# One-hots of edge places moved from the even to the odd half steps of a graph layer on one Trainium2 core

## The chip, the core and the metric

The kernel runs on one core of a Trainium2 chip. The core has five engines that run side by side: TensorE (PE in the profile, with PEld for its weight loads), VectorE (DVE), ScalarE (ACT), GpSimd (POOL) and SyncE (SP). The metric is the device time of one execution in microseconds (us). Lower is better.

## The reference

One layer of a graph network over 12,500 nodes with 128 features and 400,000 edges, which are sorted by their destination. Cut to what matters:

```python
h = relu(layernorm(x))                                  # 12500 x 128
m = relu(concat(h[src], h[dst], edge_attr) @ w1 + b1) @ w2 + b2
agg = segment_sum(m, dst, 12500)
gi, gh = agg @ w_ih + b_ih, h @ w_hh + b_hh             # a GRU cell per node
r = sigmoid(gi_r + gh_r); z = sigmoid(gi_z + gh_z); n = tanh(gi_n + r * gh_n)
out = x + (1 - z) * n + z * h
```

## The kernel before

**Tables.** A first part makes h transposed for all nodes (`hT_all`, kept in SBUF) and a table A = h @ w1[0:128] in HBM, so that the source's share of an edge's product is a row of A.

**Pairs and halves.** The 3,125 tiles of 128 edges are taken in 391 pairs `k` of up to eight tiles (two groups of four: the "double group"). Each pair is worked off in two half steps: `u = 2k` (even) and `u = 2k + 1` (odd), with four tiles each. The main loop runs over `u`, and each engine executes its instructions in the order in which this loop writes them; no scheduler moves them.

**What one pair needs.**

- Eight gathers on GpSimd (`gather`, L144), each an indirect DMA of 128 rows of A by the numbers in `src_i` into the pair's tile G. Twelve such tiles are to be had at the start and eight later; 18 of the 391 pairs are not gathered but fetched column by column out of `hT_all` by ScalarE (L775) and VectorE (L777). That makes 2,981 gathers.
- The transposed one-hot of the destination nodes (`onehot_T`, L493): VectorE compares the destination numbers of 512 edges, which a DMA has spread over 64 partitions, with each partition's node number, and writes 64x512 floats into L.
- The product of this one-hot and of the edge attributes with RW (`pre`, L590), on TensorE. RW holds the destination's share, made from a window of `hT_all` by `window` (L512, L515) and `window_rows` (L524).
- The one-hot of the edges' places in the window (`onehot`, L542): VectorE compares `dloc` (16 bits, one place per edge) with `iota` (16 bits, 0 to 31), both in SBUF, and writes 128x256 floats into one of six OH tiles.
- `add` (L615): G += product, on VectorE, once a half's four gathers have landed. `relu` (L621) on ScalarE writes RB.
- `seg` (L634) on TensorE sums RB by OH into PSUM, and `take` (L642, L643) copies the sums out.
- Every fourteen pairs, a block of 512 nodes goes through the GRU cell (`node`, L650 to L723), spread over later halves.

**The order on VectorE.** In an even half: some of the L777 copies, the copy L642 of the pair before, the compares L493 and L542 for the pair three ahead, the add L615 of the half two ahead; then L512, more L777 and the two L524. In an odd half: L777, the add L615, L777. The one-hot of places for pair k + 3, made in half 2k, is first read by `seg` in half 2k + 6.

**The order on GpSimd.** In the main part it issues gathers alone. `gathers` asks for them as far ahead as the G tiles allow.

Of the kernel before, what the change touches and what calls it, by code (L numbers as in the profile page):

```python
# [54 lines left out]
def tile_gnn(ctx: ExitStack, tc: tile.TileContext, x, src, srcT, dstT, dstP, eaT, eaP, w1, b1, w2T, b2,  # L55
# [15 lines left out]
    def tiles(k):  # L71
        return (0 if k == 0 else SUP0 + (k - 1) * PAIR, SUP0 + k * PAIR)
# [416 lines left out]
    def onehot_T(k):  # L489
        if k >= NP:  # L490
            return
        c = slice((k % QP) * 512, (k % QP + 1) * 512)
        nc.vector.tensor_scalar(Ls[k // QP][:2 * V, c], Ds[k // QP][:, c], node_of[:, k:k + 1],  # L493
                                None, op0=ALU.is_equal)
# [31 lines left out]
    def onehot(k):  # L526
        if k >= NP:
            return
        t0, t1 = tiles(k)
        OH[k] = OHB[k % len(OHB)]  # L530
        for a in range(2) if k == 0 else (None,):
            if a is None:
                o, s = OH[k].rearrange("p j a v -> p a j v"), slice(t0, t1)
                d = dloc[:, s].rearrange("p (a j) -> p a j", a=2)[:, :, :, None]
                shape = [128, 2, GRP, V]
                i = iota[:, None, None, :]
            else:
                e = min(t1, (a + 1) * GRP)
                o, d = OH[k][:, :e - a * GRP, a, :], dloc[:, a * GRP:e, None]
                shape = [128, e - a * GRP, V]  # L540
                i = iota[:, None, :]
            nc.vector.tensor_tensor(o, d.to_broadcast(shape), i.to_broadcast(shape),  # L542
                                    op=ALU.is_equal)
# [9 lines left out]
    def raw_h(u):  # L553
        if u < 2 * RAW:
            for i, s in enumerate(slots(u)):
                relu_norm(unit(u)[:, s, :], unit(u)[:, s, :], HE[u][:, i, :])

    def raw_stats(u):
        if u < 2 * RAW:
            l = slots(u)  # L560
            HE[u] = bn_sqrt(p2, bn(p2, lambda j: unit(u)[:, l[j], :], 128, len(l)), 128, len(l))

    def raw_fin(u):
        if u < 2 * RAW:
            n = len(slots(u))
            st = p2.tile([128, GRP, 2], F32, name="st_raw", bufs=4)
            bn_fin(p2, st[:, :n, :], HE[u], 128, n)
            HE[u] = st

    def raw_turn(u):  # L570
        if u < 2 * RAW:
            l = slots(u)
            pt = ps1.tile([128, 512], F32, name="misc")
            for i, s in enumerate(l):
                nc.tensor.transpose(pt[:, i * 128:(i + 1) * 128], unit(u)[:, s, :], ident)
            hT = p3.tile([128, 512], F32, name="hTe", bufs=2)
            nc.vector.tensor_copy(hT[:, :len(l) * 128], pt[:, :len(l) * 128])
            HE[u] = hT
# [3 lines left out]
    def pre(u):  # L582
        if u >= NU:
            return
        k, h = divmod(u, 2)
        PP[u] = ps2.tile([128, GRP, D], F32, name="pre")
        for i in range(2):
            c0 = (k % QP) * 512 + (2 * h + i) * 128
            raw = u in HE or k in hand
            nc.tensor.matmul(PP[u][:, 2 * i:2 * i + 2, :], Ls[k // QP][:, c0:c0 + 128], RW[k % 4],  # L590
                             start=True, stop=not raw)
            if raw:
                l = unit_tiles(u)
                for n, (t, j, a) in enumerate(l):
                    if j % 2 == i:
                        if k in hand:
                            c = (a * GRP + j) * 128
                            cols = hand[k][:, c:c + 128]
                        else:
                            cols = HE[u][:, n * 128:(n + 1) * 128]  # L600
                        nc.tensor.matmul(PP[u][:, 2 * i + a, :], cols, w1a, start=False,
                                         stop=n + 1 == len(l) or l[n + 1][1] != j)


    def add(u):
        if u >= NU:
            return
        if u in HE or u // 2 in hand:
            RT[u] = PP.pop(u)
            HE.pop(u, None)  # L610
            if u % 2:
                hand.pop(u // 2, None)
        else:
            RT[u] = unit(u)
            nc.vector.tensor_tensor(RT[u], PP.pop(u), RT[u], op=ALU.add)  # L615

    def relu(u):
        if u >= NU:
            return
        o = RB[u % 3]  # L620
        nc.scalar.activation(o[:, :, :D], RT.pop(u), AF.Relu)  # L621
        if u % 2:
            G.pop(u // 2, None)
# [207 lines left out]
    def stages(u):  # L831
        if u + 7 >= 0:
            raw_stats(u + 7)
        if u + 6 >= 0:
            raw_fin(u + 6)
            raw_h(u + 6)
        if u % 2 == 0:
            onehot_T(u // 2 + 3)
            onehot(u // 2 + 3)
        if u + 4 >= 0:  # L840
            raw_turn(u + 4)
        if u + 3 >= 0:
            pre(u + 3)
        if u + 2 >= 0:
            add(u + 2)
            relu(u + 2)

    for u in range(-7, 0):
        stages(u)
# [12 lines left out]
    for u in range(NU):  # L862
# [29 lines left out]
        if h == 0:  # L892
            take(k - 1)
        stages(u)
        other(1)
        other(2)
# [177 lines left out]
```

## Time and profile before

| | us |
|---|---|
| median of 3 runs | 3845.28 (3842.6 to 3846.54) |
| the profiled execution's own time | 3851.33 |
| its span, first to last instruction | 3849.6 |

| engine | busy us | share of the span | instructions |
|---|---|---|---|
| POOL | 2895.7 | 75% | 2989 |
| PE | 2660.6 | 69% | 13274 |
| DVE | 2007.8 | 52% | 12309 |
| ACT | 1650.1 | 43% | 11720 |

The profile shows one execution, instruction by instruction, with start and duration. "Busy" counts the instruction's own duration; what an engine spends between instructions, waiting or issuing, is listed as idle time before the next one, with what ended it. The word "issue" stands there for time in which the engine waited for nothing that the profile shows. L144 is line 144 of the kernel.

### The profile page before, as it was taken

The page shows a single profiled execution, that of the slowest core. Times are in us where ns is not written, and L with a number is a line of the kernel's source. Part 1 is how long each engine was busy: PE and PEld are TensorE (multiplying, and loading weights), DVE is VectorE, ACT ScalarE, POOL GpSimd, SP SyncE. Part 2 cuts the span into 40 slices and gives each one's busy share as a digit, 9 for nine tenths or more (in the row PEclk, how much of TensorE's full clock was granted, in tenths as well). Part 3 has the DMA queues.
Part 4 walks back from the last instruction along what each step waited for, and adds up shares of the span by engine and source line. Part 5 has one row for each costly group of instructions (what it writes and reads, how often), then busy time and mean ns, then how long its engine had stood idle before and what let it go on. Part 6 is the DMA issues. An engine that isn't in the chain of part 4 may idle for free. (4 is left out here: it accounts for less than half of the span.)

```text
span 3849.6 us, 62154 instructions
## 1 busy us (share of the span) xinstructions
PE 2660.6 (69%) x13274; PEld 1624.1 (42%) x13274; DVE 2007.8 (52%) x12309; ACT 1650.1 (43%) x11720; POOL 2895.7 (75%) x2989
## 2 busy tenths in 40 slices
PE   6688766766775675776777577666667766775776
PEld 6554443443443443443444344433434443443443
DVE  7766655544545444554555455455545545544432
ACT  5446544444444444443544444444444444444311
POOL 7777777777777777777777777777777777777774
PEclk9888777777777777776777787687867777777776
DMA  6343333333333333333333333333333333333331
GB/s 202 87 99 93 85 91 84 77 87 82 88 82 87 82 84 85 84 86 79 90 84 83 81 88 87 77 92 78 89 80 89 77 87 82 89 80 85 88 81 38
DMA packets 151695, 333.68 MB, mean 87 GB/s; under 512 B 62088, under 2 KB 68019, under 8 KB 151317
## 3 DMA queue, kind: packets, MB, share of 16 engines
q0 software_dynamic: 95392, 195.55, 20.1%
q1 hardware_dynamic: 55781, 134.06, 13.5%
q8 instruction: 110, 1.80, 0.2%
q14 instruction: 268, 2.20, 0.2%
q10 hardware_dynamic: 144, 0.07, 0.0%
HBM read 315.60 MB, written 13.84 MB: 86 GB/s over the span
## 5 line engine op out<-in xcount | busy, mean ns | idle before, releaser
L144 POOL DMA_INDIRECT G<-A,src_i x2904 | 2821.9, 972 | 886.8 <-issue 837.3
L590 PE MATMUL pre<-RW,L 128*128 128x256 f32 x3128 | 1164.7, 505 | 120.4 <-DVE G L615 107.5
L775 ACT COPY HE_act<-hT_all 128x4 uint8 x10240 | 1055.5, 188 | 380.8 <-issue 378.9
L621 ACT ACTIVATE RB<-G 128x512 f32<-128x512 f32 x726 | 456.9, 629 | 1409.2 <-DVE G L615 1099.0
L615 DVE TENSOR_TENSOR G<-pre,G 128x512 f32<-128x512 f32 x726 | 499.8, 688 | 890.4 <-DMA G<-A,src_i 876.2
L515 PE MATMUL oh<-w1b,hw 128*64 128x128 f32 x782 | 217.1, 370 | 1019.8 <-DVE hw L512 1014.0
L590 PEld LDWEIGHTS pre<-RW,L 128*128 128x128 f32 x3128 | 696.7, 246 | 435.2 <-issue 311.3
L777 DVE TENSOR_REDUCE HE_dve<-hT_all 128x4 uint8 x8192 | 641.3, 148 | 359.8 <-issue 354.2
L634 PE MATMUL seg<-RB,OH 128*32 128x129 f32 x6250 | 657.4, 346 | 6.0 <-ACT dcol L643 4.4
L515 PEld LDWEIGHTS oh<-w1b,hw 128*64 128x64 f32 x782 | 92.6, 168 | 1184.2 <-DVE hw L512 1154.0
L634 PEld LDWEIGHTS seg<-RB,OH 128*32 128x32 f32 x6250 | 356.3, 133 | 256.6 <-issue 139.9
L524 DVE TENSOR_TENSOR RW<-oh,b1b 32x128 f32<-32x128 f32 x782 | 218.9, 280 | 171.8 <-PE oh L515 164.8
L642 DVE COPY sums<-seg 64x128 f32<-64x128 f32 x391 | 108.5, 278 | 211.0 <-PE seg L634 207.1
L493 DVE TENSOR_SCALAR L<-Ld,node_of 64x512 f32<-64x512 int32 x391 | 193.9, 496 | 0.1
L643 ACT CAST dcol<-seg 64x1 f16<-64x1 f32 x391 | 59.6, 152 | 261.2 <-DVE sums L642 259.0
L665 PEld LDWEIGHTS nd<-spot,sums 64*128 64x128 f32 x782 | 164.4, 321 | 13.8 <-issue 13.8
L665 PE MATMUL nd<-spot,sums 64*128 64x40 f32 x782 | 168.5, 404 | 0.0
L542 DVE TENSOR_TENSOR OH<-dloc,iota 128x256 f32<-128x256 f16 (+1 forms) x392 | 160.0, 408 | 0.0
L629 PE MATMUL seg<-zrow 1*64 1x129 bf16 x391 | 107.1, 274 | 0.0
L512 DVE COPY hw<-hT_all 128x64 f32 x391 | 85.3, 218 | 18.2 <-issue 7.0
L144 POOL DMA_INDIRECT G<-in_x,src_i x77 | 72.8, 946 | 24.9 <-issue 22.8
L629 PEld LDWEIGHTS <-zrow 1*64 1x64 bf16 x391 | 43.6, 111 | 97.4 <-issue 97.4
(147 smaller groups left out, 1366.4 us busy)
## 6 DMA issues: line engine op xcount, KB each, us to landing
L<-in_eaP SPq DMA_DIRECT2D x195, 256.0 KB
Ld<-in_dstP SPq DMA_DIRECT2D x390, 128.0 KB
G<-A,src_i POOLq DMA_INDIRECT x2904
xb<-in_x SPq DMA_DIRECT2D x28, 256.0 KB
out<-xb SPq DMA_DIRECT2D x28, 256.0 KB
xs<-in_x SPq DMA_DIRECT2D x11, 512.0 KB
A<-asb SPq DMA_DIRECT2D x11, 512.0 KB
src_i<-in_srcT SPq DMA_DIRECT2D x19, 80.0 KB
```

What stands on the lines that cost most here:

```text
L144: nc.gpsimd.indirect_dma_start(out=G[k][:, j, a, :], out_offset=None, in_=table, in_offset=bass.IndirectOffsetOnAxis(ap=src_i[c][:, i:i + ...
L493: nc.vector.tensor_scalar(Ls[k // QP][:2 * V, c], Ds[k // QP][:, c], node_of[:, k:k + 1], None, op0=ALU.is_equal)
L515: nc.tensor.matmul(PB_[k][:2 * V, :D], hw.rearrange("p a v -> p (a v)"), w1b, start=True, stop=True)
L524: nc.vector.tensor_tensor(RW[k % 4][s, a, :], pm[s, :D], b1b[s, :], op=ALU.add)
L542: nc.vector.tensor_tensor(o, d.to_broadcast(shape), i.to_broadcast(shape), op=ALU.is_equal)
L590: nc.tensor.matmul(PP[u][:, 2 * i:2 * i + 2, :], Ls[k // QP][:, c0:c0 + 128], RW[k % 4], start=True, stop=not raw)
L615: nc.vector.tensor_tensor(RT[u], PP.pop(u), RT[u], op=ALU.add)
L621: nc.scalar.activation(o[:, :, :D], RT.pop(u), AF.Relu)
L634: nc.tensor.matmul(SEG[k][V * a:V * (a + 1), :D + 1], OH[k][:, j, a, :], RB[u % 3][:, (j % 2) * 2 + a, :D + 1], start=False, stop=all(b != ...
L665: nc.tensor.matmul(pt[:, bass.ds(offs[i], V + SHIFT)], sums[:, i, :], spot, start=False, stop=i == n - 1)
L775: nc.scalar.copy(he[:, e * 4:e * 4 + 4], h_bytes[:, bass.ds(v - H_AT, 4)])
L777: nc.vector.tensor_reduce(he[:, e * 4:e * 4 + 4], h_bytes[:, bass.ds(v - H_AT, 4), None], AX.X, ALU.max)
```

## The change

The call of `onehot` for the pair three ahead moves from the even half to the odd half of the same pair. `onehot_T` stays in the even half. Nothing is added or left out: `u // 2 + 3` is the same pair in both halves. The condition `u > -7` leaves out the half before the first pair.

```diff
         if u % 2 == 0:
             onehot_T(u // 2 + 3)
+        elif u > -7:
             onehot(u // 2 + 3)
         if u + 4 >= 0:
             raw_turn(u + 4)
```

On VectorE, L542 thus no longer follows L493 but stands behind the L524 and the L777 copies of the pair, directly ahead of the odd half's add L615 (and in the first ten pairs ahead of the copy L577 of `raw_turn`). The other engines' instructions stand in the order in which they stood.

## The prediction

> **What bounds the kernel now.** I read the page's groups first, for the engine with the least slack, then that engine's waits, then the timeline, gather by gather.
>
> ```profile
> L144 POOL DMA_INDIRECT G<-A,src_i x2904 | 2821.9, 972 | 886.8 <-issue 837.3
> ...
> L615 DVE TENSOR_TENSOR G<-pre,G 128x512 f32<-128x512 f32 x726 | 499.8, 688 | 890.4 <-DMA G<-A,src_i 876.2
> ...
> L493 DVE TENSOR_SCALAR L<-Ld,node_of 64x512 f32<-64x512 int32 x391 | 193.9, 496 | 0.1
> ...
> L542 DVE TENSOR_TENSOR OH<-dloc,iota 128x256 f32<-128x256 f16 (+1 forms) x392 | 160.0, 408 | 0.0
> ...
> L144 POOL DMA_INDIRECT G<-in_x,src_i x77 | 72.8, 946 | 24.9 <-issue 22.8
> ```
>
> POOL is "75% busy", but its idle time is nearly all "issue": about 0.30 us after every gather.
>
> ```profile
> POOL G L144 <- issue: 860.2, 2823, 0.3
> POOL G L144 <- DMA G<-A,src_i: 26.2, 86, 0.3
> ...
> POOL G L144 <- PE misc L575: 2.9, 3, 2.2
> ...
> POOL G L144 <- DMA src_i<-in_srcT: 1.8, 1, 1.8
> ```
>
> Columns: total us, times, longest. No wait is longer than that fixed 0.3 us but for one of 1.8 (the first indices) and one of 2.2 (a G tile, at 122 us). So GpSimd issues gathers without a break: the timeline has the first at 3.2 us and the last from 3807.18 to 3808.12; the rest, 41.5 us, is the last pairs' work and the last node block. The sum: 2,981 gathers of 0.941 us (the usual shortest) = 2805.1, idle 886.8 + 24.9 = 911.7, and 89.6 us by which the records exceed 0.941 us, together 3806.4; the start adds 1.4. VectorE waits 876 us for the gathers at L615 and TensorE behind it: they follow. Only the length of a gather, the number of gathers, the start and the tail set the end. The change touches no gather, so **its whole worth lies in those 89.6 us.**
>
> Where they come from: sorted by duration, 2,616 gathers take under 0.962 us and 365 take up to 1.76. The timeline shows who stands beside the long ones.
>
> ```profile
> 1291.73 1.75 POOL L144 DMA_INDIRECT G<-A,src_i  x1 [0.30 <-issue]
> 1291.86 0.47 DVE L493 TENSOR_SCALAR L<-Ld,node_of 64x512 f32<-64x512 int32 x1
> ...
> 1292.25 0.41 DVE L542 TENSOR_TENSOR OH<-dloc,iota 128x256 f32<-128x256 f16 x1
> ```
> ```profile
> 1476.87 0.47 DVE L493 TENSOR_SCALAR L<-Ld,node_of 64x512 f32<-64x512 int32 x1
> 1477.00 1.16 POOL L144 DMA_INDIRECT G<-A,src_i  x1 [0.30 <-issue]
> 1477.26 0.41 DVE L542 TENSOR_TENSOR OH<-dloc,iota 128x256 f32<-128x256 f16 x1
> ```
> ```profile
> 1689.17 0.40 DVE L542 TENSOR_TENSOR OH<-dloc,iota 128x256 f32<-128x256 f16 x1
> 1689.30 1.08 POOL L144 DMA_INDIRECT G<-A,src_i  x1 [0.30 <-issue]
> ```
> ```profile
> 1548.24 1.01 POOL L144 DMA_INDIRECT G<-A,src_i  x1 [0.30 <-issue]
> ...
> 1548.65 0.47 DVE L493 TENSOR_SCALAR L<-Ld,node_of 64x512 f32<-64x512 int32 x1
> ...
> 1549.05 0.41 DVE L542 TENSOR_TENSOR OH<-dloc,iota 128x256 f32<-128x256 f16 x1
> ```
>
> Subtract a gather's excess from the end of the VectorE instruction that blocks it. First: 1.75 - 0.94 = 0.81, L542 ends 0.93 after the gather's start, difference 0.12. Third: 0.14, L542 ends at 0.27, difference 0.12-0.13. Second: 0.22, and it is L493 that ends at 0.34: again 0.12. So a gather wants something 0.119 us after its start; if L493 or L542 runs at that moment, it waits for that instruction's end, and, behind L493, in some cases for the end of L542 too (first window). Fourth: an L493 that runs 0.82 us into the gather holds it to its own end (1549.12 - 1548.24 = 0.88, excess 0.07); L542 there does not. Over the gathers after 200 us:
>
> - L493 runs at the 0.119 us point: 103 blocked, 38.0 us. In 45 of them the wait goes on to L542's end (24.7 us).
> - L542 alone runs there: 136 blocked, 23.9 us.
> - L493 runs at the 0.82 us point: 54 blocked, 8.1 us.
> - The rest: 72 gathers with 12.7 us (node lines L713 to L717 and the start among them), and 7.0 us of spread.
>
> **The change part by part.** Numbers of instructions and durations stay: 391 L493, 392 L542, 2,981 gathers; no queue of SP, ACT, PE or POOL is reordered, and no DMA moves.
>
> *L493 loses its follower.* It is now followed by L615, one of whose inputs lies in PSUM; no long gather's wait ends with an L615. The 103 blocked gathers then wait to L493's end alone: the sum of those remainders in the trace is 23.1 us in place of 38.0. **-14.9 us.** The 8.1 us stay.
>
> *L542 at its new place.* I replayed it: in each of the 360 gathered pairs after 200 us put L542 at the end of the instruction ahead of the odd half's L615 (less the 75 ns by which such instructions overlap), and ask whether it covers a gather's 0.119 us point. It does in 140, with 28.3 us; for all 379 pairs 29.7, in place of 23.9. **+5.8 us.** At a random phase it would be 0.408² / 2 / 1.277 (mean pitch) x 379 = 24.7 us, so +0.8.
>
> Sum: -14.9 + 5.8 = -9.1 by the replay; with random phases -14.1. All phases move once the gathers shorten. A longer replay, which walks both engines through the whole trace with these blocking rules, gives 92 us of excess for the old order (trace: 89.6) and 75 to 80 for the new: -11 to -17, with some 4 us of scatter per order. I take **-12 us**.
>
> *Costs set at nothing.* L542's shift delays an odd L615 that doesn't wait by up to 0.33 us (0.41 less overlap; the odd L615 found its gather landed in 41% of pairs), and with it L777, L642 and L493 of the next pair; an even L615 comes as much earlier. Pair by pair that cancels, and the G tiles cover it: an L615 starts on average 3 to 6 us after its last gather's issue, against eight G tiles (one lasts eight gathers of 1.28 us with the idle time: 82 us in all). If that cover were gone, 380 x 0.33 = 125 us would be at stake, but the POOL waits show none. It is thin only at the start, where VectorE is up to 98 us behind: the 2.2 us wait may vanish or double, hence -2 to +3 us. The tail holds no L542 (the last starts at 3781.0, ahead of the last gather): 0. Of new waits there are none: `dloc` is made long before, and the OH tile's last reader is five halves back.
>
> **A rule against this.** The trace's row is the third window: L542, two fp16 inputs in SBUF, holds a gather for 0.14 us. The Trainium skill, "SBUF — State Buffer", section "Who interferes with whom", says that a VectorE instruction with two SBUF inputs contends with a GpSimd instruction that reads SBUF, but also that `tensor_tensor` was not seen to stall a DMA issued there, inferring that it takes only the read half of the shared ports and making descriptors needs the write half. By the latter L542 blocks nothing wherever it stands, and the change is worth 0. The windows speak for the first half (the gather reads its indices), and for the split: L542 blocks at 0.119 and never at 0.82, where L493 does. I follow the row. [...]were the gather to hold them for 0.94 us, L542 could not keep its median of 409 ns (longest 474). The trace contradicts that, so the gather's holds are short.
>
> **The rivals.**
>
> *No change (chance 0.22).* L542 falls on the index reads more often at its new place, or the 45 double blocks cost less than counted; also the case that the order of the two hardly matters. Zero gain on L493's side plus the random-phase L542 gives +0.8: 3838 to 3853, centre 3845. For it: the replay gives L542 5.8 us of the 14.9 back. Against: the double blocks are in the trace with 24.7 us.
>
> *Slower (0.09): L542 locks onto the index reads.* An L615 that waited starts within 0.2 us of a gather's start in half of the cases (211 of 414), so what follows has a preferred phase. A blocked read costs 0.2 us on average. L493's side saves 14.9, so the balance tips when L542's blocks exceed 23.9 + 14.9 = 38.8 us: 0.10 us a pair, or half of the pairs blocked where the replay has 39%. At two thirds, 379 x 0.67 x 0.2 = 51 us, it is +12: 3857. Against: L777 copies and the wait for the window's product lie between, and the replayed starts spread over all phases.
>
> *A larger gain (in the forecast's 0.69).* If L542 falls on fewer reads than at random (12 us), -27: 3818.
>
> **How the numbers follow.** A measurement of this kernel tells about 0.2%, 7.7 us, from no change. The profiled execution lies 6.0 us above the median; the difference is taken from the median: 3845.3 - 12 = 3833. The forecast (0.69, 3818 to 3837), no change (0.22), slower (0.09). The range 3820 to 3846 leaves out the slower case, half of no change's upper side and the best of the gain: 0.2. Faster 0.69, same 0.22, slower 0.09.
>
> **What would show it.** After: L144's mean falls from 972 to 968 ns (12 / 2981 = 4 ns); its idle time stays at 912 us; no gather beside L493 outlasts L493's end by 0.33 us; gathers above 1.4 us become rare; long gathers now also stand in odd halves beside L542. Wrong if L144's mean doesn't move, if POOL shows waits above 0.3 us in number, or if the time between the last gather and the end grows.

## The result, and the profile after

| | before | after |
|---|---|---|
| median of 6 runs each, us | 3843.94 (3841.85 to 3846.73) | 3812.76 (3803.85 to 3814.37) |
| ratio | | 0.9913, 95% interval 0.99 to 0.9926 |
| profiled execution: its own time, us | 3851.33 | 3807.14 |
| its span, us | 3849.6 | 3805.4 |

The change makes the kernel 31 us faster, where 12 were predicted; the range 3820 to 3846 does not hold the time. The direction was right, the size 2.6 times too small. One run further down, of `pair_to_odd_2`, fell in a slow state (4482.48 us), and ratios here leave out such runs.

The groups of the page of after (busy us, mean ns of one, idle us before them):

```profile
L144 POOL DMA_INDIRECT G<-A,src_i x2904 | 2784.3, 959 | 886.4 <-issue 838.5
...
L615 DVE TENSOR_TENSOR G<-pre,G 128x512 f32<-128x512 f32 x726 | 499.4, 688 | 867.0 <-DMA G<-A,src_i 858.1
...
L493 DVE TENSOR_SCALAR L<-Ld,node_of 64x512 f32<-64x512 int32 x391 | 194.7, 498 | 0.0
...
L542 DVE TENSOR_TENSOR OH<-dloc,iota 128x256 f32<-128x256 f16 (+1 forms) x392 | 163.9, 418 | 2.4 <-issue 0.4
...
L144 POOL DMA_INDIRECT G<-in_x,src_i x77 | 73.0, 947 | 24.9 <-issue 22.9
```

GpSimd still issues without a break. Its waits in after (us, times, longest):

```profile
POOL G L144 <- issue: 861.4, 2827, 0.3
POOL G L144 <- DMA G<-A,src_i: 23.5, 77, 0.3
...
POOL G L144 <- PE misc L575: 2.5, 3, 1.9
POOL G L144 <- DMA src_i<-in_srcT: 1.7, 1, 1.7
```

The idle time of GpSimd is the same (911.7 us before, 911.3 after, the sums of its two groups). What shrank is the gathers themselves: the mean of L144 fell from 972 to 959 ns, and the sum by which all 2,981 records exceed 0.941 us fell from 89.6 to 52.2 us. I call this sum the **excess**; it is the quantity to watch in all runs below. A gather of 0.962 us or more is called **held**; the shorter ones, which nothing holds, make 7.0 us of the excess before and 7.5 after ("spread" below). Gathers over 1.2 us went from 102 to 29, over 1.4 us from 47 to 9.

The rest of the difference between the two profiled executions lies behind the last gather: 41.4 us before, 35.1 after. The stretches there, of before and then of after (stretch, us, busy us and count of PE, PEld, DVE, ACT, POOL, granted clock, DMA share, GB/s):

```profile
3808.00:3826.00 18.00, 13.56 (x55) 8.54 (x55) 2.84 (x7) 0.83 (x3) 0.12 (x1) 0.50 0.01 4
3826.00:3850.00 24.00, 15.48 (x19) 4.40 (x18) 4.14 (x6) 1.82 (x3) 0.00 (x0) 0.50 0.04 12
```
```profile
3770.00:3788.00 18.00, 13.37 (x55) 8.54 (x55) 2.84 (x7) 0.83 (x3) 0.24 (x1) 0.50 0.01 4
3788.00:3806.00 18.00, 9.21 (x19) 2.92 (x18) 4.14 (x6) 1.82 (x3) 0.00 (x0) 0.78 0.05 16
```

The second row of each holds the same 19 matmuls. At a granted clock of 0.50 they take 15.48 us, at 0.78 they take 9.21. This is no gift of the change: the seven profiled executions below that took under 3900 us have either some 35 us there (four of them, at a clock of 0.72 in their last 23.6 us) or some 41 us (three, at 0.50), whatever they do with the one-hots. So 44.2 us of span are 37.4 of excess, 6.3 of this tail and 0.5 of other things. The medians differ by 31.2, as they would if before's median run had the short tail and after's the long one; of runs without a trace that is only inferred.

Where the excess went, by the prediction's own classes (number held, us; the first 200 us of the run stand in "the rest"):

| | before | predicted | after |
|---|---|---|---|
| L493 runs at the 0.119 us point | 103, 38.0 | 23.1 | 69, 10.3 |
| L542 alone runs there | 136, 23.9 | 29.7 | 102, 14.7 |
| L493 at the 0.82 us point | 54, 8.1 | 8.1 | 59, 9.1 |
| the rest | 72, 12.7 | 12.7 | 52, 10.5 |
| spread | 7.0 | 7.0 | 7.5 |

Both classes that the change touches came out at half of what was predicted. The prediction's rule was: if L493 or L542 runs 0.119 us after a gather's start, the gather waits for that instruction's end. Two windows of the timeline of after (start us, us, engine, line) show which gathers obeyed it and which didn't.

```profile
820.08 0.41 DVE L542 TENSOR_TENSOR OH<-dloc,iota 128x256 f32<-128x256 f16 x1
820.25 1.06 POOL L144 DMA_INDIRECT G<-A,src_i  x1 [0.30 <-issue]
```
```profile
530.74 0.28 DVE L642 COPY sums<-seg 64x128 f32<-64x128 f32 x1 [0.78 <-PE seg L634]
530.90 0.94 POOL L144 DMA_INDIRECT G<-A,src_i  x1 [0.30 <-issue]
...
530.95 0.47 DVE L493 TENSOR_SCALAR L<-Ld,node_of 64x512 f32<-64x512 int32 x1
```

In the first, L542 was already running when the gather began: it ends 0.24 us after the gather's start, less 0.12 is the excess of 0.12. As the rule has it. In the second, L493 starts 0.05 us after the gather and runs over its 0.119 us point; by the rule the gather would wait to 531.42 and take 1.34 us. It takes 0.94. Of 22 gathers in after at which L493 starts 0.01 to 0.12 us late, none is held.

### The profile page after: what moved, and what is told of

Its sections match the earlier page's. It is cut to its first block, busy times and chain, and to the rows that moved or that the text cites. A ratio compares the mean times of both kernels' runs of the same rounds, so it can differ in the third digit from the quotient of the medians.

```text
span 3805.4 us, 62155 instructions
## 1 busy us (share of the span) xinstructions
PE 2650.9 (70%) x13274; PEld 1620.3 (43%) x13274; DVE 2017.1 (53%) x12309; ACT 1648.6 (43%) x11720; POOL 2858.3 (75%) x2989
## 5 line engine op out<-in xcount | busy, mean ns | idle before, releaser
L144 POOL DMA_INDIRECT G<-A,src_i x2904 | 2784.3, 959 | 886.4 <-issue 838.5
L615 DVE TENSOR_TENSOR G<-pre,G 128x512 f32<-128x512 f32 x726 | 499.4, 688 | 867.0 <-DMA G<-A,src_i 858.1
L777 DVE TENSOR_REDUCE HE_dve<-hT_all 128x4 uint8 x8192 | 641.5, 147 | 360.9 <-issue 356.7
L524 DVE TENSOR_TENSOR RW<-oh,b1b 32x128 f32<-32x128 f32 x782 | 219.1, 280 | 181.7 <-PE oh L515 171.9
L642 DVE COPY sums<-seg 64x128 f32<-64x128 f32 x391 | 108.1, 277 | 182.6 <-PE seg L634 177.2
L493 DVE TENSOR_SCALAR L<-Ld,node_of 64x512 f32<-64x512 int32 x391 | 194.7, 498 | 0.0
L542 DVE TENSOR_TENSOR OH<-dloc,iota 128x256 f32<-128x256 f16 (+1 forms) x392 | 163.9, 418 | 2.4 <-issue 0.4
L144 POOL DMA_INDIRECT G<-in_x,src_i x77 | 73.0, 947 | 24.9 <-issue 22.9
```

The lines of the kernel that those rows point to most:

```text
L144: nc.gpsimd.indirect_dma_start(out=G[k][:, j, a, :], out_offset=None, in_=table, in_offset=bass.IndirectOffsetOnAxis(ap=src_i[c][:, i:i + ...
L524: nc.vector.tensor_tensor(RW[k % 4][s, a, :], pm[s, :D], b1b[s, :], op=ALU.add)
L777: nc.vector.tensor_reduce(he[:, e * 4:e * 4 + 4], h_bytes[:, bass.ds(v - H_AT, 4), None], AX.X, ALU.max)
```

## The experiments

Two things were open: what exactly makes an L493 or L542 hold a gather, and which part of the move (away from behind L493, out of the run that begins with the copy L642, into the odd half) brought the gain. On the three chips of eleven of the runs below, called disturbed, the unchanged kernel itself took 5277 to 5381 us, and in the traces taken there GpSimd waits for other engines, up to 32 us at a time. Those times say nothing of the change, and only durations of single gathers are read there. What disturbs these chips was not found.

The page's waits of one of them, `spacer`, show that other bound (the line numbers are one higher in this kernel):

```profile
POOL G L144 <- ACT RB L622: 1486.3, 210, 32.3
```

Excesses are therefore compared among the disturbed or among the undisturbed alone: of `run_to_odd` below it is 44.3 us disturbed and 85.0 undisturbed. Each is that of one profiled execution, and the spread in it is 6.7 to 14.3 us, as the gathers that nothing holds take 0.944 us (median) in some executions and 0.947 in others; so the tables also give the part of the held gathers (before: 82.6 us, after: 44.6).

**Is it L493 and L542 that hold the gathers?** `no_L542`, its repeat, `no_L493` and `neither` write zeros in the place of the compares.

```diff
-            nc.vector.tensor_tensor(o, d.to_broadcast(shape), i.to_broadcast(shape),
-                                    op=ALU.is_equal)
+            nc.vector.memset(o, 0.0)                       # no_L542, neither
...
-        nc.vector.tensor_scalar(Ls[k // QP][:2 * V, c], Ds[k // QP][:, c], node_of[:, k:k + 1],
-                                None, op0=ALU.is_equal)
+        nc.vector.memset(Ls[k // QP][:2 * V, c], 0.0)      # no_L493, neither
```

> The order of before, L542 replaced by a memset of the same tile (no SBUF input), so the one-hots of places are not computed: what L493 costs alone. Chain theory with a request just ahead of the gather: L493 alone costs 13 to 15 us at the read and 6 to 8 late ones; gathers' excess 38 us in place of 90, 3793 to 3798 us. The prediction's point rule: 23.1 + 8.1 us stay, excess 51 us, 3803 to 3808 us.

> The order of before, L542 replaced by a memset, so the one-hots of places are not computed: what L493 costs by itself. Run theory: excess 36 to 42 us, as the changed kernel less its L542 blocks of 12 to 15 us, 3792 to 3800 us. Point rule of the prediction: 23.1 + 8.1 us for L493, excess 51 us, 3803 to 3808 us.

> The order of before, L493 replaced by a memset of the same part of L (no SBUF input), so the transposed one-hots are not computed: what L542 costs alone. Chain theory: L542 alone costs 8 to 12 us, excess 29 us, 3782 to 3790 us. Point rule: L542 at its phases covers 164 reads of 0.207 us, 34 us, excess 54 us, 3803 to 3812 us.

> The order of before, L493 and L542 both replaced by memsets of the same tiles, so neither one-hot is computed: the floor of the gathers' excess. All theories: what is left is the spread of some 7 us, the node lines L713 to L717 with 6 to 10 us and single ones; excess 15 to 22 us, 3770 to 3778 us.

| | median us (before on that chip) | ratio, interval | excess us | of it, held |
|---|---|---|---|---|
| `no_L542` | 5391.97 (5381.19) | 1.0029, 0.9988 to 1.007 | 26.3 | 19.5 |
| `no_L542_again` | 5357.49 (5276.81) | 1.0141, 1.003 to 1.0252 | 24.8 | 18.0 |
| `no_L493` | 5268.4 (5381.19) | 0.9798, 0.9672 to 0.9925 | 127.8 | 114.6 |
| `neither` | 5378.59 (5276.81) | 1.0195, 1.0063 to 1.0327 | 21.6 | 7.3 |

With both compares gone the held gathers make 7.3 us: of 85 gathers whose 0.119 us point the memset in L493's place covers, none is held. With L493 kept and L542 gone they make 18.0 to 19.5. But with L493 gone and L542 kept the excess is **127.8 us, the largest of all runs**; no disturbed run that keeps both compares has more than 79.8. So the harm that L542 does depends on the instruction in front of it. That had to be seen undisturbed:

> L493 replaced by a memset of the same part of L, L542 directly behind it; the transposed one-hots are not computed. Run theory: the run L642, memset, L542 blocks as one piece of 0.9 us[...]; excess 120 to 130 us, slower than before: 3865 to 3890 us. Point rule of the prediction (L542 holds only a gather whose read it covers): 3803 to 3812 us.

3889.55 us against 3849.03, ratio 1.0107 (1.009 to 1.0124), excess 121.8. Slower than before, with one VectorE compare replaced by a memset. Its group of gathers, and a window of its timeline (L541 is the L542 of the others, L641 the L642):

```profile
L144 POOL DMA_INDIRECT G<-A,src_i x2904 | 2854.1, 983 | 886.6 <-issue 813.3
```
```profile
644.06 0.28 DVE L641 COPY sums<-seg 64x128 f32<-64x128 f32 x1 [0.99 <-PE seg L633]
644.29 1.68 POOL L144 DMA_INDIRECT G<-A,src_i  x1 [0.30 <-issue]
644.40 0.48 DVE L493 MEMSET L<- 64x512 f32 x1
644.81 0.35 DVE L541 TENSOR_TENSOR OH<-dloc,iota 128x256 f32<-128x256 f16 x1
```

The one-hot of places ends at 645.16, 0.87 us after the gather's start; less 0.12 that is 0.75, and the gather takes 0.94 + 0.74. The gather waits for an instruction that starts 0.52 us after it, behind a copy and a memset that by themselves hold nothing. A hold thus can begin **two instructions ahead** of the L542 that causes it: 24 of 25 gathers that began up to 0.11 us before this memset were held.

**Something between the two, or the other order.** `spacer` and `spacer_again` put a small memset between L493 and L542 in the even half; `swapped` exchanges them.

```diff
             onehot_T(u // 2 + 3)
+            nc.vector.memset(spacer, 0.0)                  # spacer: 128x96 floats of its own
             onehot(u // 2 + 3)
```
```diff
-            onehot_T(u // 2 + 3)
             onehot(u // 2 + 3)
+            onehot_T(u // 2 + 3)
```

> Both one-hots stay in the even half, with a memset of 128x96 floats (some 0.13 us, no SBUF input, a scratch tile) between L493 and L542. Chain theory (L542 queued directly behind L493 keeps the port closed across both, and parting the two is the whole of the change's gain, wherever L542 then stands): 3805 to 3820 us, the longer gathers fall from 365 to about 290 and none outlasts L493 by 0.33 us. Place theory (the odd half is what helps, because L542 meets fewer gathers there; the prediction's point rule holds): L493 loses its follower, L542 keeps its phases, about 3830 us (3825 to 3840).

> The memset of 128x96 floats between L493 and L542 in the even half, on an undisturbed chip. Run theory (a run of L642, L493 and L542 without a wait in it closes the port as one piece, from its first instruction on, and the change gains by cutting the run): the run is cut but the memset is still part of what precedes L542; gathers' excess about 50 us in place of 90, 3800 to 3815 us. Place theory (it is the odd half that helps): 3830 to 3845 us.

> L542 ahead of L493 in the even half, both still in one run behind L642. Run theory: the run is as long as before, so 3835 to 3855 us. If instead it is L542 queued behind L493 that closes the port early, the swap frees it: 3805 to 3820 us. Place theory: 3838 to 3848.

`spacer` (disturbed): 5431.41 against 5381.19, 1.0105 (0.9999 to 1.021), excess 48.5. `spacer_again`: 3829.78 against 3849.03, 0.9952 (0.9935 to 0.9968), excess 67.8. `swapped`: 3820.57 against 3849.03, 0.9925 (0.9908 to 0.9941), excess 58.8. Their groups, in this order:

```profile
L144 POOL DMA_INDIRECT G<-A,src_i x2904 | 2799.8, 964 | 887.2 <-issue 789.0
```
```profile
L144 POOL DMA_INDIRECT G<-A,src_i x2904 | 2791.1, 961 | 886.8 <-issue 810.9
```

An added instruction makes the kernel 19 us faster: once L542 doesn't stand directly behind L493, none of the 80 gathers that are held with L493 at their 0.119 us point waits on to L542's end (in before 45 of 103 do). It gains less than the change because of where L542 now falls (L494 and L543 are the compares in this kernel, L840 is the added memset):

```profile
940.71 0.95 POOL L144 DMA_INDIRECT G<-A,src_i  x1 [0.30 <-issue]
...
941.21 0.69 DVE L494 TENSOR_SCALAR L<-Ld,node_of 64x512 f32<-64x512 int32 x1
...
941.86 0.14 DVE L840 MEMSET spacer<- 128x96 f32 x1
941.93 0.35 DVE L543 TENSOR_TENSOR OH<-dloc,iota 128x256 f32<-128x256 f16 x1
941.96 1.14 POOL L144 DMA_INDIRECT G<-A,src_i  x1 [0.31 <-issue]
```

The first gather stretches L494 to 0.69 us, so that it ends 1.19 us after that gather's start, whenever it began, and L543 starts 0.03 us ahead of the next gather and holds it. 93 L494 start 0.48 to 0.73 us into a gather; 87 of the gathers that follow are held, with 17.1 us. Behind the memset, L542 holds even gathers that begin up to 0.06 us ahead of it (19 that begin 0.01 to 0.06 us ahead; their holds end with L542).

In `swapped` the two compares are still neighbours, but now L542 stands directly behind L642: an L542 that starts 0.01 to 0.12 us after the gather holds it in 18 of 18 cases, and L493 behind it in 0 of 29. So the **early hold**, one that begins before the instruction that causes it has started, belongs to L542; behind L777, L524 and the like in after, an L542 that starts 0.01 to 0.12 us after the gather holds it in 0 of 40 cases.

**Which part of the move brought the gain?** `pair_to_odd` moves both one-hots, still back to back, to the odd half. `run_to_odd` moves the copy L642 along with them, so that the run of before stands whole in the odd half. `take_behind` leaves the pair in the even half and puts L642 behind the add.

```diff
-        if u % 2 == 0:
+        if u % 2 and u > -7:                               # pair_to_odd, run_to_odd
             onehot_T(u // 2 + 3)
             onehot(u // 2 + 3)
...
-        if h == 0:
+        if h == 1:                                         # run_to_odd alone
             take(k - 1)
```
```diff
-        if h == 0:
-            take(k - 1)
         stages(u)
+        if h == 0:                                         # take_behind
+            take(k - 1)
```

In `run_to_odd` the start of a node block moves to the odd half as well, so that it still follows its sums. First the disturbed runs:

> L493 and L542 both move to the odd half, still directly behind one another, now behind L777 or L524 and not behind L642. Place theory (the odd half is what helps): as the changed kernel, 3805 to 3818 us. Run theory (L542 directly behind L493 closes the port through both): the gain is lost in the main, gathers' excess 72 to 90 us, 3830 to 3848 us, and gathers of over 1.4 us are back (before: 47, changed: 9).

> L493 and L542 move to the odd half behind L777 or L524; L642 stays in the even half. If it takes L642 at the front: the gain is there, excess 45 to 60 us, 3802 to 3818 us. If L493 directly ahead of L542 suffices: excess 72 to 90 us, 3830 to 3848 us.

> L642, L493 and L542 all move to the odd half in one run (the node blocks' start goes along by half a step). If the run behind L642 closes the port as one piece: as before, excess 80 to 95 us, 3838 to 3855 us. If the odd half is what helps: 3805 to 3818 us.

> All stay in the even half, but L642 goes behind the add L615, so L493 and L542 follow L777. If it takes L642 at the front: excess 45 to 60 us, 3802 to 3818 us. If L493 directly ahead of L542 suffices, or the even half is at fault: 3830 to 3848 us.

`pair_to_odd` takes 5319.61 us against 5276.81, ratio 1.0102, excess 32.5, and again 5448.44 against 5368.98, 1.0116, 42.0. `run_to_odd` takes 5278.15 against 5368.98, 0.981, 44.3; `take_behind` 5268.68, 0.9804, 79.8. The time goes the other way than the excess here: on a chip disturbed like this the length of the gathers doesn't set the kernel's time. Undisturbed:

> The pair in the odd half without L642: neither part by the gather records so far. Two-part theory: as the changed kernel, excess 45 to 60 us, 3803 to 3818 us, although L542 directly follows L493. If their being neighbours costs something everywhere: 3825 to 3848 us.

> L642, L493 and L542 in one run in the odd half. By the gather records so far it keeps the early hold (gathers held by an L493 that begins up to 0.14 us after their start) but gathers get in at L493's end. Two-part theory: excess 62 to 75 us, 3820 to 3834 us. The run as one piece with both parts: 3838 to 3855. Place theory: 3805 to 3818.

> The pair stays in the even half, L642 goes behind the add. No early hold, but gathers held by L493 wait on to L542's end. Two-part theory: excess 72 to 85 us, 3828 to 3842 us. If L642 at the front is the whole cause: 3802 to 3818 us.

| | median us (before: 3852.7) | ratio, interval | excess us | of it, held |
|---|---|---|---|---|
| `pair_to_odd_2` (three runs) | 3814.19 | 0.9901, 0.9874 to 0.9927 | 58.2 | 45.1 |
| `run_to_odd_2` | 3840.71 | 0.9971, 0.9956 to 0.9986 | 85.0 | 71.8 |
| `take_behind_2` | 3841.23 | 0.9971, 0.9961 to 0.9982 | 77.3 | 70.5 |

With L493 and L542 **still back to back**, `pair_to_odd_2` gains as much as the change. Taking L542 away from behind L493, the reason on which the forecast stood, is therefore not needed for the gain. Leaving the even half with L642 kept in front, or getting rid of L642 in front of the pair, each brings about a third (12.0 and 11.5 us of 38.5). One window of the timeline of each, in the table's order:

```profile
1235.12 0.95 POOL L144 DMA_INDIRECT G<-A,src_i  x1 [0.30 <-issue]
1235.17 0.47 DVE L493 TENSOR_SCALAR L<-Ld,node_of 64x512 f32<-64x512 int32 x1
1235.57 0.41 DVE L542 TENSOR_TENSOR OH<-dloc,iota 128x256 f32<-128x256 f16 x1
```
```profile
471.72 0.28 DVE L642 COPY sums<-seg 64x128 f32<-64x128 f32 x1
471.88 1.34 POOL L144 DMA_INDIRECT G<-A,src_i  x1 [0.30 <-issue]
471.92 0.47 DVE L493 TENSOR_SCALAR L<-Ld,node_of 64x512 f32<-64x512 int32 x1
...
472.32 0.41 DVE L542 TENSOR_TENSOR OH<-dloc,iota 128x256 f32<-128x256 f16 x1
```
```profile
538.80 0.47 DVE L493 TENSOR_SCALAR L<-Ld,node_of 64x512 f32<-64x512 int32 x1
538.99 1.44 POOL L144 DMA_INDIRECT G<-A,src_i  x1 [0.30 <-issue]
...
539.20 0.41 DVE L542 TENSOR_TENSOR OH<-dloc,iota 128x256 f32<-128x256 f16 x1
```

First: L493 starts 0.05 us into the gather, and nothing is held. Second: the same phase, and the same distance from L642 as in after's window at 530.90, but with L542 behind L493 the gather is held to L493's end (472.39 - 471.88 - 0.12 = 0.39, excess 0.40). Third: no L642 in front; L493 ran already, and the gather is held past L493's end (539.27) to L542's (539.61 - 538.99 - 0.12 = 0.50, excess 0.50). So there are two effects, which the counts over the traces keep apart (gathers after 200 us; in the last column those that are held with L493 at their 0.119 us point):

| | order on VectorE | early hold: L493 starts 0.01 to 0.12 us into a gather and the gather is held to its or L542's end | of gathers held with L493, those that wait on to L542's end |
|---|---|---|---|
| before | even: L642, L493, L542 | 15 of 23 | 45 of 103 |
| `run_to_odd_2` | odd: L642, L493, L542 | 18 of 22 | 9 of 116 |
| `take_behind_2` | even: L777, L493, L542 | 4 of 26 | 59 of 73 |
| `pair_to_odd_2` | odd: L777, L493, L542 | 0 of 38 | 3 of 76 |
| `spacer_again` | even: L642, L493, memset, L542 | 2 of 23 | 0 of 80 |
| `spacer` (disturbed) | the same | 8 of 16 | 0 of 82 |
| `no_L542` (disturbed) | even: L642, L493, memset | 0 of 28 | 0 of 53 |
| after | even: L642, L493, L615 | 0 of 22 | 0 of 69 |

The other disturbed runs repeat it: the hold runs on in 54 of 85 cases in `take_behind`, 1 of 45 and 3 of 55 in `pair_to_odd` and its repeat, 0 of 51 in `run_to_odd`, whose early hold is 16 of 22.

An early hold beside L493 is common only with L642 in front **and** an L542 as one of the next two instructions; with L542 third, behind a memset, it was rare in one run (2 of 23) and not in the other (8 of 16), and without an L542 it didn't occur. The hold onwards to L542's end is common only with L542 directly behind L493 in the even half; within before it occurs only where VectorE came to L642 without a pause (45 of 62 gathers, against 0 of 41 where L642 had waited). The change takes away both at once. Why the odd half lets a gather in between the two, and why L777 in front of them gives hardly an early hold where L642 does, these runs do not tell.

Not every size came as expected. `pair_to_odd_2`, `take_behind_2` and `no_L493_again` fell into the ranges named for two such effects or for a hold by the whole run. `run_to_odd_2` did not: with the onward hold nearly gone, 62 to 75 us of excess and 3820 to 3834 us were expected, and it came out at 85.0 and 3840.71, which lies in the range named for a run that holds as one piece. Of the 85.0, 13.1 are spread, 6 more than in before. `spacer_again` and `swapped` fell between the ranges of their theories, `both_after_add` below all of its own.

**A better place.** `even_after_add` leaves both in the even half with L542 behind the add, `odd_after_add` puts L542 behind the odd half's add, and `both_after_add` puts each behind an add (only the added lines are shown):

```diff
         if u + 2 >= 0:
             add(u + 2)
             relu(u + 2)
+        if u % 2 == 0:
+            onehot_T(u // 2 + 3)           # both_after_add; the others leave it ahead
+            onehot(u // 2 + 3)             # even_after_add alone
+        elif u > -7:
+            onehot(u // 2 + 3)             # odd_after_add, both_after_add
```

> L542 stays in the even half but stands behind the add L615 there, no longer behind L493. Chain theory: as the changed kernel or a few us less, 3800 to 3813 us. Place theory: an L542 in the even half keeps costing what it cost alone, 23.9 us, so 3825 to 3835 us; if it is the phase behind a gather's landing that counts, 3812 to 3820.

> As the changed kernel, but L542 behind the odd half's add L615 in place of ahead of it. An add that waited starts close behind a gather's start, so L542 ends mostly before the next gather's request: its blocks fall from 102 to about 40, from 15 to about 5 us; 3800 to 3808 us. If L542's place does not matter once it is parted from L493: 3810 to 3815 us.

> L493 stands behind the even half's add L615, L542 behind the odd half's add: neither follows the other, and neither follows L642. An add that waited starts within 0.2 us of a gather's start in half of the cases, so L542 would then end about 0.1 us before the next gather's request. Run theory: a few us below the changed kernel, 3797 to 3812 us. Place theory: as the changed kernel, 3808 to 3818 us.

Disturbed: `even_after_add` 5416.06 against 5381.19, 1.0057 (1.0007 to 1.0107), excess 37.5; `odd_after_add` 5321.99 against 5276.81, excess 29.6. Undisturbed: `both_after_add` **3792.32** (3790.95 to 3793.89) against 3849.03, ratio 0.9852 (0.9835 to 0.9868), excess 38.3. It beats both kernels: 0.9852 and the change's 0.9913 have intervals that don't meet, though the two were not run on one chip. Its groups:

```profile
L144 POOL DMA_INDIRECT G<-A,src_i x2904 | 2770.3, 954 | 886.0 <-issue 806.0
...
L493 DVE TENSOR_SCALAR L<-Ld,node_of 64x512 f32<-64x512 int32 x391 | 203.0, 519 | 0.0
```

Behind the add both meet the gathers at other moments: L542 runs at the 0.119 us point of 66 gathers (157 in after) and costs 5.3 us (14.7), L493 costs 8.5 there (10.3) and 1.9 late in the gather (9.1).

## Why the prediction was wrong

**What bounds the kernel: right.** GpSimd's issue without a break carried through: idle 911.3 us, no wait above 0.3 us but the two of 1.9 and 1.7, and the whole gain of the span outside the tail is excess.

**The step that failed** is the rule of the 0.119 us point: "if L493 or L542 runs at that moment, it waits for that instruction's end". It was read off the trace of before, where an L493 that starts shortly after a gather often did hold it, as the run L642, L493, L542 holds early. In after, without that run, an instruction holds a gather only if it was already running a few hundredths of a us ahead of the gather's record. For after the rule splits by when the instruction started (us over the gathers whose point it covers):

| started | L493: rule, measured | L542: rule, measured |
|---|---|---|
| more than 0.06 us before the gather | 11.8, 10.1 | 11.8, 11.6 |
| later (34 L493, 65 L542) | 13.1, 0.4 | 22.2, 3.4 |

The replay's phases were not at fault: by the rule, the phases that came would have made 24.9 us for L493 (predicted 23.1) and 34.0 for L542 (predicted 29.7). Had the rule held, the excess of after would have been 52.2 + 12.7 + 18.8 = 83.7 us and the gain 6 us, half of the forecast. That the replay gave 92 us for the old order, where the trace has 89.6, didn't test the rule: L493 covers 113 points in before, and 103 of these gathers are held; in after it is 69 of 116.

The trace of before already spoke against the point. Of 23 gathers at which L493 starts 0.01 to 0.12 us late, 8 are not held, though L493 covers their point; and five that L493 missed, starting 0.12 to 0.15 us after them, are held by 0.49 to 0.83 us. The prediction's first window is one of these five: the gather began at 1291.73 and L493 at 1291.86. Ahead of both stood

```profile
1291.66 0.28 DVE L642 COPY sums<-seg 64x128 f32<-64x128 f32 x1
```

The prediction's second and third windows, in which the compare starts 0.13 us ahead of the gather, fit either reading.

**L493 loses its follower: -14.9 predicted, -27.7 came** (38.0 to 10.3). The hold to L542's end is gone, as said (45 to 0). The remainder, 12.8 us below the replay, is mostly the late starters, worth 12.7. And the reason given, that L493 loses its follower, isn't what it takes: `pair_to_odd_2` keeps the follower and loses the cost (13.0 us over the points that L493 covers, 38.0 in before).

**L542 at its new place: +5.8 predicted, -9.2 came** (23.9 to 14.7). The sign was wrong for the same reason: it covers 157 points, more than the replay's 140 in 360 pairs (147 for all 379), and holds 102. Of the 23.9 us in before, moreover, 12.3 came from the fixed place that a stretched L493 gave L542, as in the window at 940.71: 99 L493 start 0.48 to 0.73 us into a gather, and 83 of the gathers that follow are held. The change parts the two and ends that.

**Late L493: right**, 8.1 predicted, 9.1 measured. So were the rest and the spread, to 2.2 and 0.5 us.

**Costs set at nothing: held.** No new wait, the G tiles cover L542's shift; the first blocks show 1.9 us where 2.2 stood. The tail shrank in the profiled run by 6.3 us, with the clock (0.78 for 0.50), and other kernels show both lengths.

**The rule against this.** The Trainium skill, "SBUF — State Buffer", section "Who interferes with whom", has that `tensor_tensor` wasn't seen to stall a DMA issued on GpSimd. The rows stand against it here more firmly than before: L542 holds gathers at its new place too (window at 820.25; 102 of 157), with L493 gone the excess is 121.8 us, more than with both, and of 97 gathers whose point the memset in L542's place covers in `no_L542`, one is held.

**The rivals.** No change fell: the excess moved by 42%. Slower fell: L542 didn't reach half of the pairs (190) with 102. The larger gain of 27 us came in size, but not for its reason, since L542 falls on more points, not fewer, than the replay gave.

**What was to be seen.** Gathers above 1.4 us rare: yes (47 to 9). Gathers that outlast L493 by 0.33 us gone: yes. Long gathers beside L542 in odd halves: yes. Idle at 912: yes. L144's mean at 968: no, 959.

## What to carry to other kernels

Where indirect gathers on GpSimd bound a kernel, sum what their records exceed the shortest by, and sort it by the VectorE instruction beside each; here 90 us hid in 2,981 gathers, and the waits of GpSimd showed none of it. A rule of blocking that is read from one order of instructions may belong to that order: before it is replayed for another, look for cases in the trace that separate "runs at that moment" from "was running before". And the best place found for such compares was apart from each other, each behind an instruction that itself waits for the gathers; where L493 and L542 stood in one run, the first could fix the second's place just ahead of a gather.

## What was not expected of the hardware

- A VectorE instruction can hold a gather before it starts: with L642 in front and L542 two instructions later, the hold began at L642 (24 of 25 in `no_L493_again`, through a memset that by itself holds none of 85 in `neither`). Replacing a compare by a memset made the kernel 40 us slower.
- Between two instructions that each hold gathers, a waiting gather isn't always let in: it waits on for the second in 45 of 103 cases in before, in 59 of 73 in `take_behind_2`, and in 3 of 76 with the pair in the odd half.
- The gather holds back, shortly: an L493 that starts 0.46 to 0.71 us into a gather that is not held ends 1.19 us after that gather's start and so takes up to 0.73 us in place of 0.47. That is where the mean of L493 in `both_after_add` comes from (519 ns against 498), and no gather pays for it there. Where L542 follows directly it fixes L542's start 0.13 us ahead of the next gather (12.3 us of the excess in before).
- The same 19 matmuls of the tail take 15.48 or 9.21 us by the granted clock, 0.50 or 0.78, in runs of the same work. The tails of these profiles differ by some six us with it.
